# Reordering the start and the end of each layer's edge train, and moving three blocks' sums of squares to VectorE, in a two-layer graph network

## The chip, the cores and the metric

The kernel runs on one core of a Trainium2 chip. The metric is the device time of one execution in microseconds. Before the change the median of three runs is 2219.21 us (2216.82, 2219.21 and 2223.94).

The engines are named as the profile names them: PE (TensorE, matrix products; PEld is its loading of weights), DVE (VectorE), ACT (ScalarE), POOL (GpSimd, which here issues the gathers) and SP (SyncE, which issues most of the other transfers). Each engine works through its own instructions in their order in the program and stops at an instruction whose operands are not ready.

## The reference

6250 nodes of 128 features, 106250 edges sorted by destination; every node has one edge to itself. Two layers, each with a layer norm and a relu before it and a residual around it:

```python
# layer 0, GATv2
xl = h @ Wl + bl;  xr = h @ Wr + br
m = leaky_relu(xl[src] + xr[dst] + edge_weight1 @ We, 0.2)
logits = m @ att
ex = exp(logits - segment_max(logits, dst)[dst])
out = segment_sum(xl[src] * (ex / segment_sum(ex, dst)[dst])[:, None], dst) + bias_out
h = batch_norm(gelu(h + out))          # mean and variance over all nodes
x = x + h

# layer 1, message passing
em = relu(layer_norm(concat(h[src], h[dst]) @ msg_w + msg_b)) * edge_weight[:, None]
messages = segment_sum(em, dst) / counts
gate = sigmoid(h @ gate_w + gate_b)
h_new = relu(layer_norm(concat(h, messages) @ upd_w + upd_b))
x = x + gate * h_new + (1 - gate) * h
```

## The kernel before

**Blocks.** Nodes lie in 49 tiles of 128 (`NT`), grouped by four (`TN`) into 13 chunks. The sorted edges are cut into `NS` = 99 blocks of `BE` = 1078. A node's edge to itself needs no gather, so `squeeze` moves the other edges together (seven steps of COPY_PREDICATED with the masks `moves`), and at most `SE` = 1024 edges, 8 tiles (`ST`), are left in a block. A block must therefore hold at least `OWN` = `BE - SE` = 54 own edges; flags computed on the chip choose a fast branch where this and some other conditions hold, and a general branch where not. The last block has 606 edges and works on `LT` = 5 tiles.

**Prologue.** The nodes are normalised in batches of three tiles (17 batches) and multiplied by the weights; `table(i)` copies a batch from PSUM into SBUF and sends its rows to `xl_d` in DRAM (L344 and L347). The first gather must wait for all of `xl_d`. DVE makes the copies of the last four batches, ACT the others.

**Layer 0.** One loop runs over rounds `s`; in round `s` a block is gathered and its logits are made, while block `u = s - LAG` (`LAG` = 7) is aggregated. For a block, POOL issues eight indirect gathers of `xl_d` rows (L187), each held back by `paced`: the first of a block waits for a mark made by the work on the block three rounds before (`PACED`). PE spreads the destination rows (`xr_d`, in a window of nodes, through a one-hot matrix) into PSUM; SP loads the window `W` and the codes `oht` for it two rounds ahead (`load`). Then L1451 adds the gathered rows, L1452 (ACT) is the relu, L1461 and L1463 weigh with `att` and sum to logits, and `lgc` (L1467) holds them. Every fourth round `maxima` takes the maxima by node of four blocks in steps: transposes on PE (`mx` L1181, `tx` L1192, L1193, L1208, L1219, L1220), scans on DVE (L1188 to L1215), exp on ACT (L1216, L1226, L1227). Seven rounds later ACT and DVE scale the gathered rows (`glw`, L1439, L1444, L1446), PE sums them by node with a one-hot matrix (`agg`, L1483), and ACT and SP store the block's partial sums to `res` (L1321).

`nodes(g)` finishes a group of nodes (13 groups, `NGR`, of 4 tiles, the last two of 3 and 2): it fetches two partial sums from `res`, multiplies the node's own row (`up`, L1246 and L1247), adds the edge to itself (L1253 to L1276), scales (L1280, ACT), blends (DVE), applies gelu (L1299, with a table load) and feeds the batch norm's statistics. It is a generator: each `yield` ends a portion, and the loop takes one portion per round. Group 10 starts in round 98, groups 11 and 12 follow; the last two are interleaved after the loop by `in_turn`. The tables `res` are zeroed by SP in rounds 0 to 4, two pieces a round.

**Middle.** Chunk by chunk over `NC` = 13 chunks: DVE applies the batch norm and the residual (`mix`, L1548), PE centres (L1553), ACT squares and splits (L1559, L1560), PE makes variances (L1584) and products (L1589), ACT the roots (L1593), DVE reciprocals (L1594) and the rows of `a_d` (`tab`, L1598). Beside it, in the first chunks, `made` makes rows of `b_d` as three bf16 parts: DVE (L1003, L1007) and ACT (L1005, L1008) take turns.

**Layer 1.** The same loop with a lag of one round: gathers of `a_d`, L1823 adds, ACT squares each tile and reads the accumulator (L1831, eight pairs a block) and takes a root (L1832), the next round's DVE scales with the reciprocal (L1857, L1844), adds a bias (L1846), ACT applies relu (L1849) and the edge weight (`glw`, L1853), PE sums by node (L1865), ACT copies (L1676), SP stores. `nodes1(g)` finishes node groups; the last two, `late` (group 11) and `last` (group 12), run portion by portion after the loop in a written order (`in_turn`).

The program keeps the order of instructions on each engine as the code issues them ("manual_schedule").

Of the kernel before, what the change touches and what calls it, by code (L numbers as in the profile page):

```python
# [9 lines left out]
F32 = mybir.dt.float32  # L10
# [7 lines left out]
P = 128  # L18
# [13 lines left out]
ST = 8  # L32
SE = ST * P
BE = 1078
# [32 lines left out]
def kernel(  # L67
# [146 lines left out]
    with tc.tile_pool(name="pre", bufs=3) as pp, tc.tile_pool(name="pre1", bufs=1) as p1, tc.tile_pool(  # L214
# [124 lines left out]
        def table(i):  # L339
            t0, k = batches[i]  # L340
            g, q = divmod(t0, PG)
            if q == 0:
                tls[g] = pp.tile([P, PG, WL], F32, name="tl")
            (V.tensor_copy if i >= n - 4 else S.copy)(tls[g][:, q : q + k, :], mms.pop(i)[:, :k, :])  # L344
            if i >= n - 3 or t0 + k == (g + 1) * PG:
                a = q if i >= n - 3 else 0
                nc.sync.dma_start(xl_d[(g * PG + a) * P : (t0 + k) * P].rearrange("(t p) f -> p t f", p=P),  # L347
                                  tls[g][:, a : q + k, :])
# [574 lines left out]
    def fast():  # L923
# [99 lines left out]
        def load_weights(s):  # L1023

            nc.sync.dma_start(ohts[s % 3][KW:P, :],
                              flat(ea_h if s < SB else ea_d, [[SE, 8], [1, SE]], s * 8 * SE))

        def one_hot_t(oht):

            return V.tensor_scalar(oht[:KW, :], oht[:KW, :], third[:KW, :], None, op0=ALU.is_equal)  # L1030
# [4 lines left out]
        with tc.tile_pool(name="col1", bufs=1) as p1, tc.tile_pool(name="ps_p", bufs=2, space=PSUM) as ps_p, tc.tile_pool(  # L1035
# [58 lines left out]
            for s in range(2):  # L1094
                load_weights(s)
                one_hot_t(wins[s][1])
            send(ea_d, 0, NS)
# [15 lines left out]

        def load(table, s, weights):
            w = load_nodes(table, s)
            if weights:
                load_weights(s)
            return w
# [40 lines left out]
        with tc.tile_pool(name="e0", bufs=2) as ep, tc.tile_pool(  # L1159
# [71 lines left out]

            def nodes(g):
# [8 lines left out]
                if last:  # L1241
                    up = ps_m.tile([P, ST, D], F32, name="m_ps")[:, :n, :]
                else:
                    up = ps_1.tile([P, TN, D], F32, name="up", tag="np")[:, :n, :]
                for j in range(n):
                    T.matmul(up[:, j, :], ones[0:1, :], blr[0:1, :], start=True, stop=False)  # L1246
                    T.matmul(up[:, j, :], h_sb[:, t0 + j, :], wlr, start=False, stop=True)  # L1247
                yield
                yield
                yield  # L1250
# [26 lines left out]
                if g >= NGR - 3:  # L1277
                    for j in range(n):
                        for o, k in ((fin[:, 1, j, :D], 1), (xl[:, j, :D], 2)):
                            S.activation(o, o, AF.Copy, scale=mm[:, k, j : j + 1])  # L1280
                    for j in range(n):
                        V.scalar_tensor_tensor(fin[:, 0, j, :D], fin[:, 0, j, :D], mm[:, 0, j : j + 1],
                                               fin[:, 1, j, :D], op0=ALU.mult, op1=ALU.add)
                    V.tensor_tensor(fin[:, 0, :n, :D], fin[:, 0, :n, :D], xl[:, :n, :D], ALU.add)
# [119 lines left out]
            turns.update({3: NCH - 3, 8: NCH - 2, 13: NCH - 1})  # L1404
            begun = breaks()
            spread(0)
            for s in range(NS + LAG + 1):
                u = s - LAG
                n = tiles(s)
                if s + 2 < NS:  # L1410
                    wins[s + 2] = load(xr_d, s + 2, True)
# [76 lines left out]
                if s < 5:  # L1488
                    zero(res0_d, WF, 2 * s)
                    zero(res0_d, WF, 2 * s + 1)  # L1490
# [32 lines left out]
        with tc.tile_pool(name="md", bufs=3) as mp, tc.tile_pool(  # L1523
# [49 lines left out]
            split(0)  # L1573
            for c in range(NC):
                cs, n = chunk(c)
                ts = slice(c * TN, c * TN + n)
                if c + 2 < NC:
                    mix(c + 2)
# [20 lines left out]
                tabs[c] = tab  # L1599
                if c:  # L1600
                    gates(c - 1)
# [16 lines left out]
        with tc.tile_pool(name="e1g", bufs=6) as gp, tc.tile_pool(name="e1", bufs=2) as ep, tc.tile_pool(  # L1618
# [187 lines left out]
            for s in range(NS + 2):  # L1806
# [14 lines left out]
                if s < NS:  # L1821
                    y = yp.tile([P, ST, D], F32, name="y")
                    added = V.tensor_tensor(y[:, :n, :], pss.pop(s)[:, :n, :], gl[:, :n, :], ALU.add)  # L1823
                    passed[s] = []
                    if s:
                        passed[s - 1].append(added)
                    ys[s] = y
                    rs = small.tile([P, ST], F32, name="rs")[:, :n]
                    sq = ep.tile([P, D], F32, name="sq1")
                    for j in range(n):  # L1830
                        S.activation(sq, y[:, j, :], AF.Square, accum_out=rs[:, j : j + 1])  # L1831
                    S.activation(rs, rs, AF.Sqrt, bias=eps, scale=1.0 / D)  # L1832
                if u >= 1:
                    flush1(u - 1)
                if 0 <= u < NS:
# [11 lines left out]
                    if s < NS:  # L1847
                        passed[s] = [marks[0], marks[-3]]
                    S.activation(yu, yu, AF.Relu)  # L1849
                    glw = glws[u % 3]  # L1850
# [8 lines left out]
                if s == NS:  # L1859
                    finish(group)  # L1860
                    next(late)
                if 0 <= u < NS:
                    aggs[u] = ps_1.tile([P, WM], F32, name="agg1_ps")
                    for j in range(m):
                        T.matmul(aggs[u], oh[:, j, :], glw[:, j, :], start=(j == 0), stop=(j == m - 1))  # L1865
                if making is not None:
                    finish(making)
                    making = None
# [69 lines left out]
```

## Time and profile before

| what | value |
|---|---|
| median of three runs | 2219.21 us |
| profiled execution, its own time | 2221.45 us |
| its span, first to last instruction | 2219.7 us |
| mean granted clock of PE | 0.656 |
| start of the first and last gather of layer 0 | 64.59, 1070.06 us |
| start of the first and last gather of layer 1 | 1173.56, 2168.16 us |
| POOL's gathers, layer 0 | 789, 971 ns each, 267.5 us idle ahead of them |
| POOL's gathers, layer 1 | 789, 956 ns each, 246.3 us idle ahead of them |
| L1844 on DVE | 789 x 340 ns |
| L1831 on ACT | 789 squares x 309 ns, 789 reads x 186 ns |

A line of the profile's groups gives the code line, the engine, the operation, what it writes and reads, how often, then the busy time, the mean of one in ns, and the idle time of the engine just before it with what ended most of it. A line of the timeline gives start and duration in us, then in brackets how long the engine had been idle and what released it. In a table of windows each engine's busy time is followed by the number of its instructions, and the last three columns are the clock granted to PE (1 is full), the mean busy share of the DMA engines, and GB/s.

### The profile page before, as it was taken

What the parts mean: (1) busy time and instruction counts of PE and PEld (TensorE: products, weight loads), DVE (VectorE), ACT (ScalarE), POOL (GpSimd) and SP (SyncE); (2) the same over time, 40 slices, a digit from 0 to 9 for tenths busy, and PEclk for the clock granted to TensorE, in tenths of its full rate; (3) what the DMA queues carried; (4) which work ended last, traced back from release to release, by engine and by line L of the source; (5) the groups of instructions that cost most, each with busy time, mean ns of one, the idle gap of its engine ahead of it and who ended that gap; (6) DMA issues with size and microseconds to landing.
All of it is one profiled execution on the core that took longest, in us unless ns stands there. A gap on an engine that the chain in (4) does not pass through costs nothing. (4 is left out here: it accounts for less than half of the span.)

```text
span 2219.7 us, 28197 instructions
## 1 busy us (share of the span) xinstructions
PE 1144.3 (52%) x6261; PEld 1020.3 (46%) x6261; DVE 1688.3 (76%) x3887; ACT 1288.3 (58%) x4330; POOL 1564.0 (70%) x1630
## 2 busy tenths in 40 slices
PE   5224555655655654645763455554554554554554
PEld 3124444544544544544652344554544554544443
DVE  8668887787787787787764677787787787887786
ACT  6224344443543444443445777777787787777785
POOL 4677777777777777777236777777777777777770
PEclk9556666566665666566776666666666666666666
DMA  5664456444435534534223343443443444343441
GB/s 143 179 181 108 108 141 179 114 95 117 111 88 115 117 82 116 120 84 108 59 61 100 89 109 93 107 109 93 107 111 95 103 114 104 92 114 93 102 112 39
DMA packets 243537, 239.21 MB, mean 108 GB/s; under 512 B 90720, under 2 KB 186921, under 8 KB 243359
## 3 DMA queue, kind: packets, MB, share of 16 engines
q0 software_dynamic: 50496, 103.92, 21.9%
q1 hardware_dynamic: 192575, 133.27, 21.6%
q8 instruction: 52, 0.85, 0.2%
q14 instruction: 126, 1.03, 0.2%
q10 hardware_dynamic: 288, 0.13, 0.0%
HBM read 189.20 MB, written 47.96 MB: 107 GB/s over the span
## 5 line engine op out<-in xcount | busy, mean ns | idle before, releaser
L187 POOL DMA_INDIRECT gl<-xl_d,src_c x789 | 766.3, 971 | 267.5 <-issue 169.7
L187 POOL DMA_INDIRECT gl<-a_d,src_c x789 | 754.5, 956 | 246.3 <-issue 178.3
L1483 PE MATMUL agg_ps<-glw,oh 128*128 128x131 f32 x1536 | 338.4, 407 | 218.7 <-ACT agg L1321 160.0
L1483 PEld LDWEIGHTS agg_ps<-glw,oh 128*128 128x128 f32 x1536 | 314.8, 310 | 239.0 <-ACT agg L1321 221.7
L1865 PE MATMUL agg_ps<-glw,oh 128*128 128x130 f32 x1040 | 235.4, 414 | 328.6 <-ACT glw L1853 320.6
L1865 PEld LDWEIGHTS agg_ps<-glw,oh 128*128 128x128 f32 x1040 | 217.8, 312 | 341.7 <-ACT glw L1853 341.7
L1831 ACT ACTIVATE sq<-y 128x128 f32<-128x128 f32 x789 | 243.8, 309 | 108.4 <-DVE y L1823 86.6
L1446 ACT ACTIVATE glw<-gl,exm 128x128 f32<-128x128 f32 x763 | 233.1, 388 | 0.0
L1452 ACT ACTIVATE m_ps<-m_ps 128x1024 f32<-128x1024 f32 (+1 forms) x99 | 99.5, 1005 | 216.2 <-DVE cc L1211 111.0
L1844 DVE SCALAR_TENSOR_TENSOR y<-y,rs,cst 128x128 f32<-128x128 f32 x789 | 211.6, 340 | 0.0
L1451 DVE TENSOR_TENSOR m_ps<-m_ps,gl 128x1024 f32<-128x1024 f32 (+1 forms) x99 | 121.6, 1229 | 117.4 <-DMA gl<-xl_d,src_c 102.9
L1865 PE MATMUL agg_ps<-ea_r,oh 128*128 128x130 f32 x512 | 117.9, 420 | 169.9 <-ACT ea_r L1853 161.5
L1132 PEld LDWEIGHTS <-oht 128*128 128x128 bf16 (+1 forms) x1578 | 144.0, 125 | 122.5 <-issue 52.0
L1865 PEld LDWEIGHTS agg_ps<-ea_r,oh 128*128 128x128 f32 x512 | 108.9, 318 | 176.2 <-ACT ea_r L1853 176.2
L1030 DVE TENSOR_SCALAR oht<-oht,third 120x1024 bf16<-120x1024 bf16 x198 | 100.1, 506 | 101.8 <-DMA oht<-dl_d 101.7
L1853 ACT ACTIVATE glw<-y,ew_c 128x128 f32<-128x128 f32 x528 | 161.5, 388 | 0.0
L1461 DVE TENSOR_TENSOR m_ps<-m_ps,att 128x1024 f32<-128x1024 f32 (+1 forms) x99 | 120.8, 1220 | 36.5 <-ACT m_ps L1452 35.6
L1831 ACT ACTIVATION_READ_ACCUMULATOR sq<-y 128x1 f32 x789 | 146.9, 186 | 0.0
L1823 DVE TENSOR_TENSOR y<-y_ps,gl 128x1024 f32<-128x1024 f32 (+1 forms) x99 | 119.5, 1207 | 33.9 <-PE agg_ps L1865 18.2
L1132 PE MATMUL m_ps<-W,oht 128*128 128x128 bf16 x789 | 88.8, 281 | 99.9 <-DVE lr L1463 94.9
L1849 ACT ACTIVATE y<-y 128x1024 f32<-128x1024 f32 (+1 forms) x99 | 104.3, 1054 | 36.3 <-DVE y L1846 36.3
L1463 DVE TENSOR_REDUCE lr<-m_ps 128x8 f32<-128x1024 f32 (+1 forms) x99 | 120.8, 1220 | 3.4
(348 smaller groups left out, 2227.5 us busy)
## 6 DMA issues: line engine op xcount, KB each, us to landing
oht<-dl_d SPq DMA_DIRECT2D x198, 240.0 KB
gl<-xl_d,src_c POOLq DMA_INDIRECT x789
gl<-a_d,src_c POOLq DMA_INDIRECT x789
res<-zt SPq DMA_DIRECT2D x20, 327.5 KB
res<-zt SPq DMA_DIRECT2D x20, 325.0 KB
res<-agg SPq DMA_DIRECT2D x99, 64.5 KB
res<-agg SPq DMA_DIRECT2D x99, 64.0 KB
W<-xr_d SPq DMA_DIRECT2D x198, 30.0 KB
```

What stands on the lines that cost most here:

```text
L187: return GP.indirect_dma_start(out=dest, out_offset=None, in_=table, in_offset=bass.IndirectOffsetOnAxis(ap=idx, axis=0))
L1132: T.matmul(ps[:, j, :], oht[:rows_, j * P : (j + 1) * P], w[:rows_, j // TN, :], start=True, stop=True)
L1446: S.activation(glw[:, j, :D], glu[:, j, :D], AF.Copy, scale=f)
L1451: passed[s] = [V.tensor_tensor(ps, ps, gl[:, :n, :D], ALU.add)]
L1461: passed[s].append(V.tensor_tensor(ps, ps, over_tiles(att8, n), ALU.mult))
L1463: V.tensor_reduce(lr, ps, AX.X, ALU.add)
L1483: T.matmul(aggs[u], oh[:, j, :], glw[:, j, :], start=(j == 0), stop=(j == m - 1))
L1823: added = V.tensor_tensor(y[:, :n, :], pss.pop(s)[:, :n, :], gl[:, :n, :], ALU.add)
L1831: S.activation(sq, y[:, j, :], AF.Square, accum_out=rs[:, j : j + 1])
L1844: marks.append(V.scalar_tensor_tensor(yu[:, j, :], yu[:, j, :], ru[:, j : j + 1], mg_ps, op0=ALU.mult, op1=ALU.mult))
L1853: S.activation(glw[:, j, :D], yu[:, j, :], AF.Copy, scale=ew_c[:, u, j : j + 1])
L1865: T.matmul(aggs[u], oh[:, j, :], glw[:, j, :], start=(j == 0), stop=(j == m - 1))
```

## The change

Seven edits in one. (1) `BE` 1079 in place of 1078: 99 blocks still, 508 edges in the last block, four tiles rather than five. (2) `table`: DVE copies batches 13 and 14, ACT the last two. (3) The load for round 2 is issued in the prologue, ahead of the three writes of `ea_d`; the zeroing of `res` starts one round later. (4) Drain of layer 0: group 10 starts in round 99 and yields twice rather than three times before its first sums; a new `lift` holds the products for the nodes' own rows, which groups 11 and 12 make in rounds 100 and 101 in another PSUM tile; these two groups yield once more behind the copies L1280. (5) Middle: `mix` of a chunk is issued behind the rows of the chunk three before, ahead of the `made` step, rather than at the head of the chunk two before. (6) Last three blocks of layer 1: one Square over the whole tile into the PSUM tile that held the spread rows, the sums by a tensor_reduce on DVE behind L1846, the root behind the relu. (7) The first portion of `late` after the loop's gathers comes behind block 98's sums on PE rather than ahead of them.

```diff
-BE = 1078
+BE = 1079
...
-            (V.tensor_copy if i >= n - 4 else S.copy)(tls[g][:, q : q + k, :], mms.pop(i)[:, :k, :])
+            (V.tensor_copy if n - 4 <= i < n - 2 else S.copy)(tls[g][:, q : q + k, :], mms.pop(i)[:, :k, :])
...
+            wins[2] = load(xr_d, 2, True)
             send(ea_d, 0, NS)
...
+            def lift(g, up):
+                t0, n = G0[g], GS[g]
+                ups[g] = up[:, :n, :]
+                for j in range(n):
+                    T.matmul(up[:, j, :], ones[0:1, :], blr[0:1, :], start=True, stop=False)
+                    T.matmul(up[:, j, :], h_sb[:, t0 + j, :], wlr, start=False, stop=True)
...
-                if last:
-                    up = ps_m.tile([P, ST, D], F32, name="m_ps")[:, :n, :]
-                else:
-                    up = ps_1.tile([P, TN, D], F32, name="up", tag="np")[:, :n, :]
-                for j in range(n):
-                    T.matmul(up[:, j, :], ones[0:1, :], blr[0:1, :], start=True, stop=False)
-                    T.matmul(up[:, j, :], h_sb[:, t0 + j, :], wlr, start=False, stop=True)
-                yield
-                yield
-                yield
+                if g not in ups:
+                    lift(g, ps_1.tile([P, TN, D], F32, name="up", tag="np"))
+                up = ups.pop(g)
+                yield
+                yield
+                if g < NGR - 3:
+                    yield
...
                             S.activation(o, o, AF.Copy, scale=mm[:, k, j : j + 1])
+                    if g >= NGR - 2:
+                        yield
...
+            if NS - 1 in due:
+                due[NS] = due.pop(NS - 1)
...
-                if s + 2 < NS:
+                if 0 < s < NS - 2:
                     wins[s + 2] = load(xr_d, s + 2, True)
...
-                if s < 5:
-                    zero(res0_d, WF, 2 * s)
-                    zero(res0_d, WF, 2 * s + 1)
+                elif s - NS in (1, 2):
+                    lift(NGR - 3 + s - NS, ps_m.tile([P, ST, D], F32, name="m_ps"))
+                if 1 <= s < 6:
+                    zero(res0_d, WF, 2 * s - 2)
+                    zero(res0_d, WF, 2 * s - 1)
...
+            mix(2)
             for c in range(NC):
...
-                if c + 2 < NC:
-                    mix(c + 2)
...
                 tabs[c] = tab
+                if c + 3 < NC:
+                    mix(c + 3)
...
-                    for j in range(n):
-                        S.activation(sq, y[:, j, :], AF.Square, accum_out=rs[:, j : j + 1])
-                    S.activation(rs, rs, AF.Sqrt, bias=eps, scale=1.0 / D)
+                    if s < NS - 3:
+                        sq = ep.tile([P, D], F32, name="sq1")
+                        for j in range(n):
+                            S.activation(sq, y[:, j, :], AF.Square, accum_out=rs[:, j : j + 1])
+                    else:
+                        S.activation(sums, y[:, :n, :], AF.Square)
+                    if s < NS - 3:
+                        S.activation(rs, rs, AF.Sqrt, bias=eps, scale=1.0 / D)
...
+                    if NS - 3 <= s < NS:
+                        V.tensor_reduce(rs, sums, AX.X, ALU.add)
                     S.activation(yu, yu, AF.Relu)
+                    if NS - 3 <= s < NS:
+                        S.activation(rs, rs, AF.Sqrt, bias=eps, scale=1.0 / D)
...
                     finish(group)
-                    next(late)
                 if 0 <= u < NS:
                     aggs[u] = ps_1.tile([P, WM], F32, name="agg1_ps")
                     for j in range(m):
                         T.matmul(aggs[u], oh[:, j, :], glw[:, j, :], start=(j == 0), stop=(j == m - 1))
+                if s == NS:
+                    next(late)
```

More of the change, by code (lines that the diff above doesn't have):

```diff
@@ L1026, in load_weights, with load @@
                               flat(ea_h if s < SB else ea_d, [[SE, 8], [1, SE]], s * 8 * SE))
+        def load(table, s, weights):
+            w = load_nodes(table, s)
+            if weights:
+                load_weights(s)
+            return w
         def one_hot_t(oht):
@@ L1112, in constants @@
             return [t[:, k * P : (k + 1) * P] for k in range(n)]
[L1114 to L1118, printed above, removed]
         def paced(s, j, row, passed):
@@ L1230, in maxima @@
                 yield
+            ups = {}
+            def lift(g, up):
[4 more added lines that the diff above has]
+                    T.matmul(up[:, j, :], h_sb[:, t0 + j, :], wlr, start=False, stop=True)
             def nodes(g):
@@ L1822, in fast @@
                     y = yp.tile([P, ST, D], F32, name="y")
-                    added = V.tensor_tensor(y[:, :n, :], pss.pop(s)[:, :n, :], gl[:, :n, :], ALU.add)
+                    sums = pss.pop(s)[:, :n, :]
+                    added = V.tensor_tensor(y[:, :n, :], sums, gl[:, :n, :], ALU.add)
                     passed[s] = []
@@ L1828, in fast @@
                     rs = small.tile([P, ST], F32, name="rs")[:, :n]
-                    sq = ep.tile([P, D], F32, name="sq1")
-                    for j in range(n):
-                        S.activation(sq, y[:, j, :], AF.Square, accum_out=rs[:, j : j + 1])
-                    S.activation(rs, rs, AF.Sqrt, bias=eps, scale=1.0 / D)
+                    if s < NS - 3:
[6 more added lines that the diff above has]
+                        S.activation(rs, rs, AF.Sqrt, bias=eps, scale=1.0 / D)
                 if u >= 1:
```

## The prediction

> **What bounds the kernel now.** I read the page's engine totals first, then its costliest groups, then POOL's timeline for the ends of the two gather trains, then the three stretches that lie outside the trains.
>
> ```profile
> PE 1144.3 (52%) x6261; PEld 1020.3 (46%) x6261; DVE 1688.3 (76%) x3887; ACT 1288.3 (58%) x4330; POOL 1564.0 (70%) x1630
> ...
> L187 POOL DMA_INDIRECT gl<-xl_d,src_c x789 | 766.3, 971 | 267.5 <-issue 169.7
> L187 POOL DMA_INDIRECT gl<-a_d,src_c x789 | 754.5, 956 | 246.3 <-issue 178.3
> ```
>
> DVE has the largest share, yet POOL's gathers set the pace. Per gather there is 0.95 us of work and 0.30 us of gap, always. 789 x 0.305 = 241 us of the 267.5 and 246.3 us of idle is that gap; what is left, 27 us and 5 us, is the wait ahead of the first gather of each layer. So in neither layer does any other engine hold POOL up. POOL's timeline gives the borders:
>
> ```profile
> 64.59 1.32 POOL L187 DMA_INDIRECT gl<-xl_d,src_c  x1 [27.41 <-DVE first_i L1050]
> ...
> 131.60 0.94 POOL L187 DMA_INDIRECT gl<-xl_d,src_c  x1 [0.30 <-issue]
> ...
> 1070.06 0.94 POOL L187 DMA_INDIRECT gl<-xl_d,src_c  x1 [0.30 <-issue]
> ...
> 1173.56 1.02 POOL L187 DMA_INDIRECT gl<-a_d,src_c  x1 [5.27 <-ACT cst L1111]
> ...
> 2168.16 0.94 POOL L187 DMA_INDIRECT gl<-a_d,src_c  x1 [0.30 <-DVE y L1844]
> ```
>
> Prologue to 64.6; layer 0's train to 1071; drain and middle, 102.6 us, to 1173.6; layer 1's train to 2169; drain to 2219.7. The sums are made on this execution: 2221.45 us in all, of which 1.75 lie around the span. It is 2.2 us above the median of 2219.21, so I carry differences over to the median. 0.3% of it, 6.7 us, is about what a measurement of this kernel can tell from no change (its three runs lie 7.1 us apart).
>
> **1. Table copies (prologue).** The last two batches of `xl_d` rows are copied from PSUM by DVE, between two long operations on edges.
>
> ```profile
> 58.48 0.56 DVE L344 COPY tl<-mm 128x387 f32<-128x387 f32 x1
> ...
> 60.21 0.28 DVE L344 COPY tl<-mm 128x129 f32<-128x129 f32 x1
> ```
>
> The last one ends at 60.49; its write takes about 3 us to land, and the first gather starts at 64.59. ACT's timeline is empty from 56.36 to 60.49, and PE has the two products by 57.0 and 57.9. On ACT the last copy can end near 58.3, the write lands near 61.4, and the first gather starts near 62.4: 2.2 us earlier (1.7 to 2.3: both writes then share the DMA). Batches 13 and 14 stay on DVE, which lies behind nothing new. This moves the train's start, not yet the end.
>
> **2. First rounds (SP's queue).** `load(xr_d, 2)` goes ahead of the three `ea_d` writes, and the zeroing of `res` one round later. DVE waits in the first rounds:
>
> ```profile
> 128.74 0.49 DVE L1030 TENSOR_SCALAR oht<-oht,third 120x1024 bf16<-120x1024 bf16 x1 [12.22 <-DMA oht<-dl_d]
> ```
>
> POOL does not see this: by `paced`, the gather at 131.60 (third of round 6) waits for round 3's L1461, which ends near 130.4, 1.2 us before. With POOL 2.2 us earlier, 1.0 us would be lost; with one load (4 DMAs) out of the loop and ahead of about 2.8 us of writes and four `zero` DMAs, the `oht` of these rounds lands several us earlier and restores the cover. So 0, and +1.0 if the cover is gone. The `ea_d` writes, now later by the load (about 4 us), are first read in round 4 and later. Zeroing ends in round 5; the first store comes in round 8.
>
> **3. One own edge more per block.** BE 1079 leaves 508 edges for the last block: 4 tiles, one gather less per layer. Every block needs at least 55 own edges to fit 1024 rows; I counted the inputs: the poorest block has 59, so the fast branch stays. In layer 0 the last add, now at 1073.44 behind the last gather, becomes bound by DVE's own queue, and gains 0.4 from the gather and 0.4 from the narrower tile ahead of it, not 1.25. In layer 1 DVE is a whole round behind POOL at the end (the last add is at 2181.9, the last gather lands near 2171): the missing gather is worth nothing by itself. A rule speaks against an odd BE. The row first: the mask `moves`, 99x1078 to bytes, takes 0.71 us. The Trainium skill ("Vector Engine (DVE) Microarchitecture Reference", 5.1) ties the two-port mode to an even outermost count, or counts equal in source and destination. If the odd width fell to one result per cycle (1.19 ns per column, as L1451's 1.22 us for 1024), each mask would take 1.28, and seven would cost 7 x 0.57 = 4.0 us. I take 0: source and destination have the same count, and DVE waits 3.71 us for PE near 51.6, behind these masks, which would cover the rest.
>
> **4. Layer 0's drain.** Through 1 and 3 its first results come 3.0 us earlier. In their way now stands `lift(10)`. Before, PE did these matmuls ahead of the last `maxima`, beside DVE's scans:
>
> ```profile
> 1079.71 0.75 PE L1247 MATMUL up<-wlr,h_sb 128*128 128x128 f32 x2
> ...
> 1081.93 3.86 PE L1483 MATMUL agg_ps<-glw,oh 128*128 128x131 f32 x16
> 1085.72 0.23 PE L1208 MATMUL tx<-ident,crow 1*21 1x1 f32 x2
> ```
>
> ```profile
> 1085.99 0.15 DVE L1211 COPY cc<-tx 21x2 f32<-21x2 f32 x1 [1.47 <-PE tx L1208]
> ```
>
> The order of instructions on PE becomes: agg(92), lift(10), L1208. PE takes them in order, so L1208, for which DVE and then ACT's exp and every later `glw` wait, stands behind 3.86 us and then eight matmul pairs: 1076.83 to 1080.3, 3.4 us. The 3.0 are used up: cc comes at about the old time, within 0.4. Were the pairs at the low clock, as earlier rows show (0.73 each, 5.8 us), +2.4; were agg(92) to start late anyway, so that the lift fell in a gap, -3.0. Behind it nothing moves: `fetch(11)` still waits for agg(96)'s store and ends in DVE's wait at 1109.87. What gains is the end: ACT does `nodes(12)`'s four copies (1.2 us) ahead of Gelu's table load (1.28) and gelu(11) rather than behind them, so DVE's blend and the last gelu come about 1.0 earlier. Layer 0 ends at -1.0; of the lift I credit a sixth (-0.5), so -1.5, from -3.8 to +1.
>
> **5. Middle.** `mix(c+3)` moves ahead of `made`'s step on DVE, so this step of c=1, 2, 3 comes one mix (0.65 us) later. ACT stands waiting for exactly these:
>
> ```profile
> 1140.40 0.62 ACT L1005 CAST tab_p<-tab_x 128x512 bf16<-128x512 f32 x1 [1.99 <-DVE tab_x L1003]
> ...
> 1144.42 0.62 ACT L1005 CAST tab_p<-tab_x 128x512 bf16<-128x512 f32 x1 [1.99 <-DVE tab_x L1007]
> ...
> 1148.42 0.62 ACT L1008 CAST tab_p<-tab_x 128x512 bf16<-128x512 f32 x1 [1.98 <-DVE tab_x L1007]
> ```
>
> Behind each cast on ACT stand square, split and sqrt, which PE's next var waits for: 3 x 0.65 = +1.95, unless the earlier mix lets PE's centring run ahead, which helps PE, not ACT. What could give it back is the clock:
>
> ```profile
> 1150.00:1153.00 3.00, 2.81 (x17) 2.59 (x17) 2.42 (x9) 1.97 (x7) 1.56 (x1) 0.74 0.46 155
> 1153.00:1156.00 3.00, 3.00 (x15) 1.97 (x14) 1.42 (x4) 0.92 (x2) 0.92 (x1) 0.69 0.50 150
> ```
>
> The last columns are granted clock, DMA share and GB/s: the clock falls to 0.74 and 0.69, and var to var takes 4.37 us here (1150.41 to 1154.78) against 2.64 later. The Trainium skill ("TensorE: Matmul & The Clock Gate", "What's actually happening") gives full rate after about 3.4 us of sustained work and takes it away after an idle window as long. By that rule there is no dip without such a gap; one dip less is worth -1.7, and the part stands near +0.2. The trace disagrees: PE's gaps ahead of the dip are under 1 us (2.36 of 3 us busy). By the trace the dip is as likely to stay, and the part is +1.95. I lean to the trace and take +1.2.
>
> **6. Last three blocks of layer 1, and the late group.** Each block's ACT work goes from 8 squares with their accumulator reads (2175.79 to 2179.3, 3.48 us) to one Square over the tile (1.06, by the relu of the same size): -2.4. DVE gets a reduce (1.22, as L1463) behind L1846, and the sqrt comes after it, so the reciprocal and the eight L1853 scalings of block 97 wait: glw(97) +1.45. DVE idled only 1.27 at this place (2179.57), so the reduce is not free. PE then has agg(98) ahead of the late group:
>
> ```profile
> 2194.24 1.60 PE L1708 MATMUL nt<-ident,fin 128*128 128x128 f32 x3 [2.69 <-issue]
> 2195.63 2.37 PE L1865 MATMUL agg_ps<-ea_r,moves 128*128 128x130 f32 x10
> ```
>
> PE stood idle 2.69 us waiting for DVE's `fin`, with agg(98)'s operands ready from about 2193.3. Swapped, and with 4 tiles, agg(98) ends some 2.3 earlier; less 1.45 for the squares, -0.95. From -2.5 (ACT's relief reaches glw) to +0.7 (the reduce is paid twice).
>
> **Sum.** Layer 0's end -1.5, middle +1.2, tail -0.95: -1.25. The good ends of the unknowns reach further (-8.2 in all, rival A) than the bad ones (+1.0 + 1.95 + 0.7 = +3.65), so I place the likeliest at -2.2: 2217.0 us.
>
> **Rivals.** *A, the head-room reaches the end.* The lift falls in a gap (layer 0 ends at -4.0), the mix is covered and the clock's dip is gone (-1.7), ACT's relief reaches the tail (-2.5): -8.2, 2211.0. For it: ACT waited 5.01 us for agg(92) at 1085.83. Against it: PE's order puts the lift before L1208. *B, slower: the clock falls in the middle.* The mix order breaks up PE's work and more chunks run at the low clock, 1.73 us each. Part 5 then costs 1.95 + 1.73n; with 2.45 gained elsewhere it passes +6.7 at n = 4.2. At five chunks +8.2: 2227.4. For it: the dip comes with DMA at 0.46 to 0.50 as the table is written. Against it: from 1156 the clock is 1.00 and ACT waits for PE only 1.14 a chunk. *C, the change does not do what it says:* the general branch is taken, far slower; the counted edges speak against it.
>
> **How the numbers follow.** Main case 0.55 (of it 0.15 faster than the bound, 0.37 within, 0.03 slower); A 0.28 (0.26 faster, 0.02 within); B 0.15 (0.12 slower, 0.03 within); C 0.02 (0.01 each within and slower). Faster 0.41, within 0.43, slower 0.16. The range reaches from -10 (A, and 2 us of the runs' spread) to +4.8 (the bad ends of the main case, and 1 us of spread): 2209 to 2224, leaving out most of B.
>
> **What would show it.** The first `xl_d` gather at 62.4; 788 gathers; cc (L1211, 21x2) within 0.5 of 1086; the last gelu 1 us earlier; ACT's waits at L1005 and L1008 grown to 2.6; agg(98) ahead of nt, the copy of mT near 2197 less the shift. Wrong if POOL's gaps exceed 0.30 in either train, if cc comes 2 us earlier (A), or if var to var takes over 4 us past 1156 (B).

## The result and the profile after

The changed kernel takes 2224.73 us (median of 20 runs, 2221.61 to 2228.79), the kernel before 2218.00 (20 runs, 2214.66 to 2223.94): 1.0030 times as long, interval 1.0023 to 1.0036, 6.7 us slower. The forecast was 2217.0 with a range of 2209 to 2224. In three of the later sets of runs the kernel before itself took 25 to 27% longer (2773 to 2814 us, with longer gather trains), so every time below stands beside the kernel before in its own set, and from those three sets only rows of one stage are compared.

Totals and gathers, from the page of the kernel after:

```profile
PE 1144.2 (51%) x6255; PEld 1019.0 (46%) x6255; DVE 1690.3 (76%) x3887; ACT 1283.2 (58%) x4291; POOL 1557.3 (70%) x1628
...
L187 POOL DMA_INDIRECT gl<-xl_d,src_c x788 | 764.7, 970 | 267.5 <-issue 171.9
L187 POOL DMA_INDIRECT gl<-a_d,src_c x788 | 750.3, 952 | 245.8 <-issue 175.9
```

One gather fewer in each layer, and POOL's gaps are as before. POOL's timeline of the kernel after gives the borders:

```profile
64.62 1.21 POOL L187 DMA_INDIRECT gl<-xl_d,src_c  x1 [27.57 <-DVE first L1053]
...
1068.31 0.94 POOL L187 DMA_INDIRECT gl<-xl_d,src_c  x1 [0.30 <-issue]
...
1183.63 1.02 POOL L187 DMA_INDIRECT gl<-a_d,src_c  x1 [5.25 <-ACT cst L1118]
...
2173.50 0.94 POOL L187 DMA_INDIRECT gl<-a_d,src_c  x1 [0.30 <-issue]
```

The parts of the profiled executions, in us. "Drain 0" runs from the start of the last gather of layer 0 to the ACT root behind the last gelu (L1301 before, L1311 after), "middle" from there to the first gather of layer 1, "drain 1" from the last gather to the end of the span.

| kernel | first gather | train 0 | drain 0 | middle | train 1 | drain 1 | span |
|---|---|---|---|---|---|---|---|
| before | 64.6 | 1005.5 | 57.3 | 46.2 | 994.6 | 51.5 | 2219.7 |
| after | 64.6 | 1003.7 | 63.3 | 52.1 | 989.9 | 49.2 | 2222.7 |
| no_drain | 63.8 | 1003.6 | 59.5 | 49.5 | 994.1 | 49.6 | 2220.0 |
| no_mix | 64.7 | 1003.8 | 62.6 | 44.3 | 990.9 | 50.4 | 2216.8 |
| no_drain_mix | 64.0 | 1004.0 | 59.6 | 46.2 | 990.6 | 50.7 | 2215.2 |
| only_drain | 63.9 | 1004.7 | 61.3 | 44.1 | 995.0 | 49.9 | 2219.0 |
| lift10_matched | 64.1 | 1003.9 | 59.8 | 46.2 | 992.3 | 49.1 | 2215.4 |
| yield_third | 64.8 | 1001.7 | 58.0 | 44.2 | 990.7 | 50.0 | 2209.4 |

Drain 0 and the middle grew by 5.9 us each. Train 1 and drain 1 gave 7.1 back in this pair, but train 1 moves by 4 us between kernels that don't differ in it (no_drain 994.1, no_drain_mix 990.6), and this execution of the kernel before is 3.5 us above its median. Two places of loss follow, and one where a gain was forecast and did not come.

The drain, on PE's timeline of the kernel after:

```profile
1078.16 0.39 PE L1182 MATMUL mx<-ident,lgc 128*20 128x128 f32 x1 [0.53 <-ACT exm L1227]
1080.55 0.18 PE L1193 MATMUL tx<-ident,fw 20*1 20x20 f32 x1 [2.00 <-DVE fw L1189]
...
1080.98 3.86 PE L1495 MATMUL agg_ps<-glw,oh 128*128 128x131 f32 x16
1084.77 0.75 PE L1240 MATMUL up<-blr,ones 1*128 1x128 f32 x2
...
1088.37 0.19 PE L1209 MATMUL tx<-ident,crow 1*20 1x1 f32 x2
```

and on DVE's:

```profile
1088.61 0.15 DVE L1212 COPY cc<-tx 20x2 f32<-20x2 f32 x1 [5.04 <-PE tx L1209]
```

The order is the forecast one, agg(92), lift(10), then the transposes of crow. But agg(92) starts at 1080.98, 0.95 earlier than before (1081.93), not 3.0, and DVE waits 5.04 us for `cc`, which comes 2.6 us later than before. Ahead of it, where the products used to be, PE now stands idle for 2.00 us. Counted from the last gather, cc comes at 20.3 us (before 15.9), and from cc to the root behind the last gelu it takes 43.0 us (before 41.4), although the extra yield of edit 4 shortens that stretch, as the runs below show.

What lengthens the stretch behind cc is the next lift, of group 11, which lies ahead of agg(94) and runs at a granted clock of 0.50 (PE's timeline, then ACT's):

```profile
1094.67 0.79 PE L1240 MATMUL m_ps<-blr,ones 1*128 1x128 f32 x2
...
1098.87 3.69 PE L1495 MATMUL agg_ps<-glw,oh 128*128 128x131 f32 x16
```

```profile
1102.64 0.27 ACT L1331 COPY agg<-agg_ps 128x131 f32<-128x131 f32 x1 [3.84 <-issue]
1102.81 0.40 ACT L1288 ACTIVATE fin<-fin,mm 128x128 f32<-128x128 f32 x1
```

ACT stands idle for 3.84 us and then copies agg(94), which ended on PE at 1102.56; its copies for group 10 (L1288) come behind that.

The middle, on ACT's timeline of the kernel after:

```profile
1147.45 0.62 ACT L1005 CAST tab_p<-tab_x 128x512 bf16<-128x512 f32 x1 [2.65 <-DVE tab_x L1003]
...
1152.13 0.62 ACT L1005 CAST tab_p<-tab_x 128x512 bf16<-128x512 f32 x1 [2.66 <-DVE tab_x L1007]
...
1156.79 0.62 ACT L1008 CAST tab_p<-tab_x 128x512 bf16<-128x512 f32 x1 [2.64 <-DVE tab_x L1007]
```

The waits grew from 1.99 to 2.65, as forecast. On PE the late casts open two gaps of 1.45 us, where the kernel before has none over 0.64 in the same chunks (first line, L1553; the others are the kernel after):

```profile
1149.11 1.12 PE L1553 MATMUL ctr<-x_sb,cen 128*128 128x512 f32 x2 [0.64 <-DVE x_sb L1548]
...
1154.12 1.05 PE L1597 MATMUL var_ps<-avg,sq 128*128 128x1 f32 x8 [1.45 <-ACT std_c L1606]
...
1158.78 1.05 PE L1597 MATMUL var_ps<-avg,sq 128*128 128x1 f32 x8 [1.45 <-ACT std_c L1606]
```

The rest is the clock; windows of 3 us (after the busy times: granted clock, DMA share, GB/s):

```profile
1152.00:1155.00 3.00, 1.55 (x10) 0.88 (x8) 0.91 (x5) 2.02 (x5) 1.56 (x1) 1.00 0.23 69
1155.00:1158.00 3.00, 2.30 (x12) 1.28 (x11) 1.75 (x4) 1.21 (x3) 0.57 (x1) 1.00 0.28 87
1158.00:1161.00 3.00, 2.22 (x17) 2.13 (x17) 2.06 (x7) 2.34 (x7) 0.99 (x1) 0.91 0.40 131
1161.00:1164.00 3.00, 3.00 (x10) 1.97 (x9) 1.79 (x5) 0.95 (x2) 0.95 (x1) 0.50 0.54 174
1164.00:1167.00 3.00, 3.00 (x12) 2.51 (x12) 1.82 (x6) 0.66 (x3) 0.61 (x1) 0.50 0.01 1
```

PE is busy 1.55 to 2.30 of 3 us while it waits for the late casts, and then the clock is 0.50 for over 6 us. By the starts of the variances (L1597 after, L1584 before), chunks 0 to 3 take 11.53 us (before 9.16), chunks 3 to 6 take 13.30 (11.90), chunks 6 to 12 take 16.57 (14.43). The late casts lie in the second stretch, the longer low clock in the third and at the end of the second. The first stretch's 2.4 us are low clock at the start, and it is not the edit that brings them: the step from chunk 0 to chunk 1 took the same 5.13 us in with_lift10, with_yield, yield_again and best_filled, which have the old mix order, and 3.02 us or less in no_drain, mix_filled and mix_filled45, which have the new one.

The prologue: the first gather did not move. Windows of 1 us of the kernel after, and then of the kernel before:

```profile
58.00:59.00 1.00, 0.00 (x0) 0.00 (x0) 0.97 (x2) 0.07 (x1) 0.00 (x0) 0.50 1.13 236
59.00:60.00 1.00, 0.00 (x0) 0.00 (x0) 0.88 (x1) 0.00 (x0) 0.00 (x0) 0.50 1.35 177
60.00:61.00 1.00, 0.00 (x0) 0.00 (x0) 0.00 (x0) 0.00 (x0) 0.00 (x0) 0.50 0.91 114
61.00:62.00 1.00, 0.00 (x0) 0.00 (x0) 0.00 (x0) 0.00 (x0) 0.00 (x0) 0.50 0.22 31
```

```profile
59.00:60.00 1.00, 0.00 (x0) 0.00 (x0) 1.00 (x2) 0.00 (x0) 0.00 (x0) 0.60 0.41 57
60.00:61.00 1.00, 0.00 (x0) 0.00 (x0) 0.49 (x2) 0.30 (x1) 0.00 (x0) 0.50 0.76 189
61.00:62.00 1.00, 0.00 (x0) 0.00 (x0) 0.00 (x0) 0.00 (x0) 0.00 (x0) 0.50 0.40 76
```

SP issues the last write 2.2 us earlier (issues end at 58.67, before at 60.86), but the writes then run into one another: the DMA share is 1.13 and 1.35 while the rate falls from 236 to 177 GB/s. The traffic thins out in the microsecond from 61 us in both kernels. PE, whose wait is put down to these writes, goes on at 62.94 (before 62.68). What holds it, and DVE and ACT with it (63.76 and 63.62 in the kernel after, put down to "issue"), for the one to two us behind the traffic is not shown.

### The profile page after: what moved, and what is told of

Read it like the earlier page. It is cut to its first block, busy times and chain, and to the rows that moved or that the text cites. A ratio compares the mean times of both kernels' runs of the same rounds, so it can differ in the third digit from the quotient of the medians.

```text
span 2222.7 us, 28139 instructions
## 1 busy us (share of the span) xinstructions
PE 1144.2 (51%) x6255; PEld 1019.0 (46%) x6255; DVE 1690.3 (76%) x3887; ACT 1283.2 (58%) x4291; POOL 1557.3 (70%) x1628
## 5 line engine op out<-in xcount | busy, mean ns | idle before, releaser
L1848 ACT ACTIVATE sq<-y 128x128 f32<-128x128 f32 x768 | 237.4, 309 | 104.9 <-DVE y L1839 83.1
L1871 ACT ACTIVATE y<-y 128x1024 f32<-128x1024 f32 (+1 forms) x99 | 104.2, 1052 | 42.4 <-DVE y L1866 42.4
```

## Experiments: which edit costs

Each kernel is the changed one with edits taken back (numbers as in the change).

no_drain takes back edit 4, no_mix edit 5, no_drain_mix both, only_drain has edit 4 alone on the kernel before:

```diff
 # no_drain
-                if g < NGR - 3:
-                    yield
+                yield
...
-                    if g >= NGR - 2:
-                        yield
...
-            if NS - 1 in due:
-                due[NS] = due.pop(NS - 1)
...
-                elif s - NS in (1, 2):
-                    lift(NGR - 3 + s - NS, ps_m.tile([P, ST, D], F32, name="m_ps"))
...
 # no_mix
-            mix(2)
...
+                if c + 2 < NC:
+                    mix(c + 2)
...
-                if c + 3 < NC:
-                    mix(c + 3)
```

> The changed kernel with its fourth edit (drain of layer 0: group 10's round, lift, the extra yield) as before. Theory 1: the profile after shows layer 0's last gelu 4.2 us later although the last gather starts 1.75 us earlier, 5.95 us in all, because lift(10) stands before L1208 on PE. Then the distance from the last gather to the last gelu falls by 5 to 6 us, cc (L1211) comes near 1084, and the whole is 4 to 6 us faster than the changed kernel: near 2219. Theory 2 (the drain is late for another reason, the four-tile block or the SP order): the distance stays, the whole stays within 1.5 us of 2224.7.

> The changed kernel with its fifth edit (mix behind the rows) as before. Theory 1: three casts (L1005, L1008) wait 0.66 us longer each, 1.95 us, and the broken-up work of PE costs the rest of the middle's 5.88 us in low clock: the middle (last gelu to first gather of layer 1) falls by 4 to 6 us, the whole to about 2219.5. Theory 2: only the casts are the edit's, the clock is set by when PE happens to start: the middle falls by 2 us, the low-clock chunks stay, the whole near 2222.5.

> The changed kernel without its fourth and fifth edit. Theory 1: both losses are gone, what stays are the gains: one gather less per layer (the train of layer 0 ends 1.75 us earlier) and layer 1's drain 2.35 us shorter: 3 to 4 us under the kernel before, near 2214. Theory 2 (the clock decides): within 2 us of the kernel before.

> The kernel before with the fourth edit alone. Theory 1: cc (L1211) comes 3 to 4 us later than before (eight products of 0.42 us lie ahead of it with no earlier start to pay for them), the last gelu about 5 us later, the whole near 2223. Theory 2 (the lift falls in a gap of PE): within 1.5 us of the kernel before.

The kernel before took 2217.17 us in this set.

| kernel | median, us | ratio to before | interval |
|---|---|---|---|
| no_drain | 2220.01 | 1.0014 | 1.0007 to 1.0021 |
| no_mix | 2217.72 | 1.0006 | 0.9998 to 1.0014 |
| no_drain_mix | 2214.84 | 0.9992 | 0.9983 to 1.0001 |
| only_drain | 2220.81 | 1.0017 | 1.0007 to 1.0026 |

The two edits make the loss, and they add: against 1.0030 for the whole change (from its own set, above), taking back the drain is worth 0.0016 (3.6 us), the mix 0.0024 (5.3 us), both 0.0038 (8.4 us). The other five edits together are worth -0.0008, which is not told from no change. In the table of parts drain 0 is 61.3 to 63.3 us with edit 4 and 57.3 to 59.6 without; the middle is 49.5 and 52.1 with edit 5 and 44.1 to 46.2 without. So theory 1 holds in kind each time, but not in its sizes: the drain of no_drain is 3.7 us shorter than that of the kernel after, where I had 5 to 6, and only_drain is 3.6 us slower than the kernel before, where I had about 6.

## Experiments: the clock in the middle

mix_filled is the changed kernel with eight unused matmul passes on PE, ahead of the variances of chunks 3 and 4; mix_filled45 has them ahead of those of 4 and 5:

```diff
                     centre(c + 1)
+                if c in (3, 4):          # mix_filled45: (4, 5)
+                    b_product(ps_b.tile([P, TN, D], F32, name="b_ps"), 0)
                 var = ps_v.tile([P, TN], F32, name="var_ps")
```

> The changed kernel with eight matmul passes more on PE (1.05 us, an unused product into the idle b_ps bank) ahead of the variances of chunks 3 and 4, where PE stands idle 1.45 us in it. Theory 1 (the later casts open gaps on PE, and the granted clock falls after them): the clock stays at 1.00 past these chunks, the middle is 3 to 4 us shorter although PE does more, near 48.5, and the whole is about 3 us under the changed kernel. Theory 2 (the low clock has nothing to do with the gaps): the middle stays at 50 to 52 us or grows.

> The changed kernel with the eight unused matmul passes ahead of the variances of chunks 4 and 5, where PE's two idle gaps of 1.45 us are (mix_filled had them one chunk too early: it closed one gap, the other stayed, and the low clock came behind it). Theory 1 (the gaps bring the low clock): the clock stays at 1.00 behind chunk 5, var to var 2.64 us there, the middle near 46.3 (44.3 and the three late casts' 1.95) unless its start is late in the clock, the whole 3 us under the changed kernel, 4 us over the kernel before. Theory 2 (the low clock comes whatever PE does): the middle 49.5 to 52.

mix_filled took 2812.71 beside 2813.83, ratio 0.9988 (0.9965 to 1.0011), mix_filled45 2772.25 beside 2774.11, 0.9997 (0.9981 to 1.0014).

mix_filled missed: I had put the filling one chunk too early. One gap was shortened to 0.25 us, the next stayed at 1.45, and the clock went to 0.50 right behind it; the middle was 49.6. In mix_filled45 both gaps hold the filling (PE's timeline, L1530, and its windows):

```profile
1396.01 1.05 PE L1530 MATMUL b_ps<-w,h_sb 128*128 128x128 f32 x8
1397.62 1.05 PE L1599 MATMUL var_ps<-avg,sq 128*128 128x1 f32 x8 [0.55 <-ACT std_c L1608]
...
1400.67 0.95 PE L1599 MATMUL var_ps<-avg,sq 128*128 128x1 f32 x8
```

```profile
1396.00:1399.00 3.00, 2.45 (x21) 2.25 (x20) 1.31 (x6) 2.97 (x8) 1.56 (x1) 1.00 0.42 143
1399.00:1402.00 3.00, 2.96 (x20) 2.29 (x20) 2.53 (x7) 1.27 (x3) 1.07 (x1) 1.00 0.32 96
1402.00:1405.00 3.00, 3.00 (x24) 2.52 (x23) 2.33 (x6) 1.86 (x7) 2.47 (x2) 1.00 0.35 107
```

The casts wait 2.65 us as in the changed kernel, PE does 2.1 us more, and the middle is 46.4 rather than 52.1 or 49.5: 44.3 of no_mix and the casts' 2. The clock stays at 1.00. The writing of the table is not enough to lower it: in no_mix the DMA share is 0.67, above the 0.54 of the kernel after, and no low clock follows:

```profile
1152.00:1155.00 3.00, 2.45 (x13) 1.63 (x14) 1.56 (x7) 3.00 (x8) 1.41 (x1) 1.00 0.67 217
1155.00:1158.00 3.00, 2.96 (x21) 2.29 (x20) 2.58 (x8) 1.24 (x4) 1.16 (x2) 1.00 0.28 91
```

Over all profiles: with the new order and at least one gap of 1.45 us left open (after, no_drain, mix_filled) a low stretch of about two chunks comes each time and costs 2.6 to 3.3 us beside the steps of mix_filled45; with the old order and gaps of up to 0.64 us one of about one chunk and 1.4 us comes behind chunk 5 in four of fifteen profiles (before, no_drain_mix, lift10_matched, lift10_again), beside the steps of no_mix. By these counts the gaps make the low clock likelier and longer, and the old order is not free of it. That filling both gaps prevents it rests on the one profile of mix_filled45.

## Experiments: the parts of the drain

From no_drain_mix, with parts of edit 4 put back: with_lift10 (group 10 in round 99, two yields), with_lift1112 (the lifts of groups 11 and 12 in rounds 100 and 101), with_yield (the extra yield behind L1288). Each was run twice, in two of the sets with long trains; no_drain_mix itself (base_again) was run in the third, so the rows below compare profiles of different sets.

> no_drain_mix with group 10 started in round 99 and two yields (of the fourth edit this part alone). Theory 1 (lift(10) ahead of L1208 is what costs): cc 3 to 4 us later than in no_drain_mix (1085.5), the drain (last gather to the root behind the last gelu) 3.5 to 4.5 us longer than 59.6, the whole near 2218.5. Theory 2 (the later groups' lifts cost): the drain within 0.7 us, the whole within 1.5 us of 2214.8.

> no_drain_mix with the products of groups 11 and 12 made in rounds 100 and 101 (of the fourth edit this part alone). Theory 1: PE is not late there, the drain within 0.7 us of 59.6. Theory 2: it is this part that costs: agg(94) and agg(95) stand behind it, the drain 3 to 4 us longer, the whole near 2218.5.

> no_drain_mix with the extra yield of groups 11 and 12 behind L1288 (of the fourth edit this part alone). Theory 1: ACT's copies of group 12 come ahead of the gelu's table load: the drain 0.7 to 1.0 us shorter than 59.6, the whole near 2214. Theory 2: no change in either.

> The kernel of with_lift10 once more, for the same reason. Theory 1 (lift(10) ahead of L1208 is what costs): the drain 3.5 to 4.5 us longer than the 59.7 of no_drain_mix, cc 20.5 to 21.5 us behind the last gather rather than 17.5, the whole 1 to 2 us over the kernel before. Theory 2 (the cost is in groups 11 and 12): the drain within 0.7 us of 59.7, the whole 2 us under the kernel before.

> The kernel of with_lift1112 once more, for the same reason. Theory 1: the drain within 0.7 us of 59.7, the whole 2 us under the kernel before. Theory 2: the drain 3 us longer and the whole 1 us over the kernel before.

> The kernel of with_yield once more, since in its set the kernel before itself took 2814 us. no_drain_mix (2214.8 beside a before of 2217.2, drain 59.7) with the extra yield behind L1288. Theory 1: the drain 0.7 to 1.0 us shorter, the whole 3 to 4 us under the kernel before. Theory 2: no change against no_drain_mix.

> no_drain_mix once more, to stand beside the next two in one set. Both theories: the whole 1 to 4 us under the kernel before; on a chip where the kernel before takes about 2217, cc 17 to 18 us behind the last gather and the drain near 59.7.

| kernel | ratio to before (interval) | cc after last gather, us | drain 0, us | cc to root, us |
|---|---|---|---|---|
| with_lift10 | 0.9998 (0.9973 to 1.0024) | 31.2 | 73.6 | 42.4 |
| lift10_again | 1.0009 (0.9989 to 1.0029) | 34.6 | 77.6 | 43.0 |
| with_lift1112 | 0.9972 (0.9948 to 0.9997) | 28.6 | 73.8 | 45.2 |
| lift1112_again | 0.9993 (0.9977 to 1.0009) | 29.4 | 75.9 | 46.5 |
| with_yield | 0.9950 (0.9927 to 0.9972) | 29.3 | 69.8 | 40.4 |
| yield_again | 0.9993 (0.9977 to 1.0009) | 29.3 | 68.8 | 39.5 |
| base_again | 0.9979 (0.9957 to 1.0002) | 28.8 | 70.3 | 41.5 |

The times do not tell these apart: the same kernel gave 0.9950 and 0.9993. The rows do: lift(10) delays cc by 2.4 to 5.8 us against base_again, the later lifts don't delay cc but lengthen the stretch from cc to the root by 3.8 to 5.0, and the yield shortens it by 1.0 to 2.0. But with_lift10 is no clean test. Edit 4 lets groups 11 and 12, like group 10, yield twice rather than three times before their first sums. Without the extra yield to make up for it this alters how `in_turn` shuffles them: their exp then falls behind a gelu, and there are two table loads more, as ACT's timeline of lift10_later shows:

> no_drain_mix with group 10 started in round 99 as the fourth edit has it, but its products one portion later on PE, behind L1208 and agg(93). Theory 1 (it is the place of the lift ahead of L1208, not the late start of group 10): cc comes as in base_again, within 0.5 us, and the drain is within 1 us of it. Theory 2 (group 10 is late whatever PE does first): cc as in base_again, but the drain 3 to 5 us longer.

```diff
+                if g == NGR - 3:
+                    yield
                 if g not in ups:
                     lift(g, ...)
                 up = ups.pop(g)
                 yield
-                yield
+                if g != NGR - 3:
+                    yield
...
```

```profile
1365.28 1.28 ACT L1310 ACT_TABLE_LOAD   x1
...
1368.20 1.28 ACT L1280 ACT_TABLE_LOAD   x1
...
1373.09 1.28 ACT L1310 ACT_TABLE_LOAD   x1
```

lift10_later has these loads too (drain 72.9, ratio 1.0020, 0.9998 to 1.0042) and so leaves its question open; it shows only that with the products behind agg(93) cc is not late (27.6 us). The closest pair is lift10_matched against yield_third. Both have the extra yield and the same table loads; they differ in the start of group 10 and in the two or three yields of groups 11 and 12, which come behind cc:

> The kernel of with_yield (no fifth edit; the extra yield of groups 11 and 12) with group 10 started in round 99, so that its products lie between agg(92) and L1208 on PE, and with the portions of groups 11 and 12 in the order of the changed kernel: with_lift10 and lift10_later lacked the extra yield, and their traces show two loads of an activation table more in the drain. Theory 1 (the place of lift(10)): beside yield_third cc is 3.5 to 5 us later behind the last gather and the drain 3 to 5 us longer, the whole 3 to 5 us. Theory 2 (the extra table loads made with_lift10's cost): cc later, but the drain within 1.5 us.

> The kernel of with_yield, as the partner of lift10_matched in one set, and the version that the experiments point to (the changed kernel without the fifth edit and without the lifts of the fourth). Both theories: 2 to 5 us under the kernel before, cc 17 to 18 us behind the last gather where the kernel before takes 2217, 29 where it takes 2770.

The kernel before took 2213.51 in this set; lift10_matched 2216.86 (1.0010, 1.0000 to 1.0020), yield_third 2214.18 (0.9999, 0.9989 to 1.0009). PE's timeline of yield_third, then of lift10_matched:

```profile
1078.66 0.27 PE L1182 MATMUL mx<-ident,lgc 128*20 128x128 f32 x1
...
1080.18 3.86 PE L1492 MATMUL agg_ps<-glw,oh 128*128 128x131 f32 x16
1083.97 0.20 PE L1209 MATMUL tx<-ident,crow 1*20 1x1 f32 x2
```

```profile
1079.75 3.86 PE L1495 MATMUL agg_ps<-glw,oh 128*128 128x131 f32 x16
1083.54 0.60 PE L1240 MATMUL up<-blr,ones 1*128 1x128 f32 x2
...
1086.99 0.19 PE L1209 MATMUL tx<-ident,crow 1*20 1x1 f32 x2
```

Behind the last gather (1066.52 and 1067.99) agg(92) starts at 13.7 and 11.8 us: without the products ahead of `mx` it comes 1.9 earlier, but they then take 3.45 between agg(92) and L1209. cc is 1.5 us later (17.7 and 19.2), the drain 1.9 longer; from cc to the root they take 40.3 and 40.6 us. So theory 1 holds in kind, at about half its size, in one profile of each; the times differ by 2.7 us, with intervals that overlap.

no_mix is lift10_matched with the lifts of groups 11 and 12 in rounds 100 and 101; its drain is 62.6, another 2.8 us. PE's timeline of no_mix:

```profile
1084.57 0.79 PE L1240 MATMUL up<-blr,ones 1*128 1x128 f32 x2
...
1090.36 0.20 PE L1209 MATMUL tx<-ident,crow 1*20 1x1 f32 x2
...
1096.47 0.48 PE L1240 MATMUL m_ps<-blr,ones 1*128 1x128 f32 x2
...
1098.87 1.97 PE L1495 MATMUL agg_ps<-glw,oh 128*128 128x131 f32 x16
```

These 2.8 us are not the later lifts. lift(10) ran at a clock of 0.50 and took 5.8 us (3.45 in lift10_matched), cc came 22.1 us behind the last gather rather than 19.2, and from cc to the root no_mix takes 40.5 us, lift10_matched 40.6. lift(11), at the full clock, took 2.4 us here, and agg(94) came 8.3 us behind cc rather than 6.5, which cost nothing; only_drain shows the same (40.5 us). By the times, too, no_mix (1.0006) is not slower than lift10_matched (1.0010). In the kernel after it is the other way round: lift(10) took 3.6 us, then lift(11) ran at 0.50 and took 4.2, agg(94) came 10.3 us behind cc, and the stretch to the root took 43.0. So lift(10) costs in every profile that has it ahead of L1209, more at the low clock, and lift(11) only where the low clock falls on it. What decides which of them it falls on is not shown.

## Experiments: the prologue, and a best version

> The kernel before with the second edit alone (ACT copies the last two batches). Theory 1 (as predicted): first gather of layer 0 near 62.4 and the whole 2 us faster. Theory 2 (the writes' own transfers end when they ended before): first gather at 63.7 to 64.7 as in all profiles so far, with the edit (62.4 to 65.1) and without it (63.9, 64.6), the whole within 1 us of the kernel before.

table_only is the kernel before with edit 2. First gather at 64.0, ratio 1.0007 (0.9989 to 1.0024). Over all 18 profiles with the edit it lies between 62.4 and 65.1, 64.0 in the mean, and at 63.9 and 64.6 in the two without. A gain of 2.2 us is not there.

> no_drain_mix with the extra yield of groups 11 and 12 and four unused matmul passes (0.5 us) ahead of the variances of chunks 4 and 5, in PE's gaps of 0.64 us. Theory 1: no low clock in the middle, which is 44.3 to 44.6 us in every profile rather than 44.1 to 46.2; drain 0.7 us shorter: 4 to 5 us under the kernel before. Theory 2 (neither tells): as base_again within 1.5 us.

best_filled is no_drain_mix with the extra yield and half as much filling ahead of chunks 4 and 5. 2763.82 beside 2773.24, ratio 0.9975 (0.9950 to 1.0000). Its drain is 1.5 us shorter than base_again's, as hoped, but its middle is 47.3: the low clock lay at the start of the middle, where nothing is filled. base_again gave 0.9979 in the same set. yield_third, which was to be 2 to 5 us under the kernel before, came out level with it (0.9999). No version is shown to beat the kernel before beyond doubt.

## Why the prediction was wrong

**Table copies: failed.** I took the write's 3 us from issue to landing as a latency that follows the issue. But the four writes, issued closer together, share the DMA, and their traffic thins out in the same microsecond as before; the wait behind it did not shrink either. -2.2 became 0. The first results of the drain, which were to come 3.0 us earlier, came 0.95 earlier, about the 0.8 that I had from the last block alone.

**First rounds, BE.** The train of layer 0 took 1.8 us less for one gather of 1.25, and POOL's gaps stayed; nothing was lost there. The masks `moves` at the odd width of 1079 take 0.72 us each in the median, as at 1078. As forecast.

**Drain: the step that failed most.** The order on PE and its link to `cc` were read rightly, but I set a head start of 3.0 against lift(10)'s 3.4. The head start was 0.95, and cc came at +2.6, not within 0.4. Second, I priced lift(11) at nothing, as "Behind it nothing moves"; in the kernel after it ran at the low clock, held agg(94) up, and cc to root took 43.0 us rather than the 40.5 of no_mix and only_drain. Third, the low-clock price of lift(10) (5.8 us) was written down as a bound and given no weight; it is what no_mix and only_drain show. The extra yield gave 1.0 to 2.0 us where I had 1.0. Layer 0 ended at +4.2, not -1.5.

**Middle: the right term, mis-sized.** The three casts' 0.65 us each are in the trace to the hundredth. I set against them the hope that the low clock might go, +1.2 in all, and gave its longer stay no weight in the likeliest sum. Instead it grew from about 1.4 us to 3.1 with PE's longer gaps, and the part measured +5.9; the 2.4 us of the slow start in it are bad luck, since kernels with the old order have it too. One low stretch gone was also worth less than my 1.7: I compared its 4.37 us with the 2.64 of later chunks, but the same step takes 3.05 without it (no_mix). The Trainium skill ("TensorE: Matmul & The Clock Gate", "What's actually happening") takes the full rate away after an idle window of about 3.4 us, and by that I had the part near +0.2. Here gaps of 1.45 us were enough, so the measurement decides.

**Tail.** mT is copied 29.3 us after the last gather (before 30.0): -0.8 in this pair, where I had -0.95, but that agreement is luck. The other kernel with the old tail (only_drain) has 28.6, and those with the new one and short trains lie between 27.7 and 30.4, so a gain of edits 6 and 7 is not shown. And I had the missing gather as worth nothing, so that the end would have come later behind the last gather; it did not (drain 1 is 49.1 to 50.7 us with 788 gathers, 49.9 and 51.5 with 789). Layer 1 gave back more than I had, by an amount that the spread of its train hides.

**Rivals.** B had the mechanism, the clock falling because the mix order breaks up PE's work, but I asked it alone for five chunks. About two chunks, the late casts and a slow start were enough together with the drain, which I had entered as a gain. By the medians the two losses are independent and add; the forecast had the one as a gain and the other as +1.2.

## What to carry to other kernels

Before moving work out of an idle stretch of an engine that takes its instructions in order, ask what stands behind its new place: the same matmuls that were free beside a scan are on the chain one instruction later. A wait added to a chain can count twice, as time and as a gap for PE's clock: look at the granted clock behind it. Before counting on a transfer to land earlier because it is issued earlier, read the DMA share and the rate of the stretch, not only the time from issue to landing: here 2.2 us at the issue were worth nothing behind other writes.

## What was not expected of the hardware

PE's granted clock fell to 0.50 after two gaps of 1.45 us, 4.7 us apart, with PE busy 1.55 and 2.30 of 3 us, and stayed there for 6 us of unbroken work; in mix_filled one such gap and one of 0.25 us were enough, and with 1.05 us of unused matmuls in each gap the clock did not fall (mix_filled45, one profile). The eight products of lift(10) took 3.45 us in lift10_matched, where the clock was 1.00 for most of them, and 5.8 us in no_mix at 0.50. What sets whether the clock is low at the start of the middle (chunk 0 to chunk 1 5.1 us in after and with_yield, 3.0 or less in before and yield_third) stays open.
